# Three edits to a fused convolution and attention block on one core: the order of small steps at the front, the last eviction of a convolution by images, and tiles of their own for the input side during attention

## The chip, the core and the metric

The kernel runs on one core of one Trainium2 chip. The metric is the device time of one execution in microseconds; the time before is 2306.33 us, the median of three runs (2305.39 to 2307.38). All data are float32.

## The reference

The input x has 8 images of 512 channels and 32 x 32 points. A group normalisation (32 groups of 16 channels) comes first, then a block with N = 2 bottlenecks, and x is added to the result. C is 256, there are 4 heads of 64 channels, `cbs` is a convolution, a batch normalisation with given statistics and a silu.

```python
t = cbs(x, cv1_w, cv1_bn, 0)                      # 1x1, 512 -> 512
ys = [t[:, :C], t[:, C:]]
for i in range(N):
    yi = ys[-1]
    z = cbs(yi, m_cv1_w[i], m_cv1_bn[i], 1)       # 3x3, 256 -> 256
    z = bot_attention(z, m_qkv_w[i], m_rw[i], m_rh[i])
    z = silu(bn_eval(conv2d(z, m_cv2_w[i], 0), m_cv2_bn[i]))
    ys.append(yi + z)
return cbs(concatenate(ys, axis=1), cv2_w, cv2_bn, 0)
```

`bot_attention` projects z to q, k and v, adds a position term `rw + rh` to k, and takes a softmax over the 1024 points of an image for each head: `softmax(q (k + r) / 8) v`.

## The kernel before

Images are handled in four pairs (p = 0 to 3), image a and image b of a pair. For a pair and each of the two bottlenecks n, one 3x3 convolution covers both images; then the attention of image a runs, then that of image b. Behind the attention of one pair lie the group normalisation and the first convolution (cv1) of the next pair; the last convolution (cv2) closes a pair.

**Order of the instructions.** The program is written stage by stage, and a planner puts each engine's instructions in an order before the run: an instruction written earlier goes first where it is ready in the planner's own model of time. [...] `tc.issue_after(ins)` adds an edge: what is written under it comes after `ins` on the engine of `ins`. Tiles of one tag share a fixed number of places (`bufs`); a new tile waits until the readers of the tile whose place it takes are done, DMAs among them.

**Front** (lines 1507 to 1594). The statistics of the first image's channels come in two parts: `bn_stats` on VectorE (`gn_stats`, L653) for the first half, and ScalarE passes with an accumulator (`stats_by_act`, L686) for the second half and for the whole second image. The three small steps between those passes (L700, L702, L703: the mean, and both sums divided by 1024) run on VectorE. `group_norm_part` (L705) then averages over groups on TensorE (gm_ps, gv_ps), forms gr and shift on VectorE and GpSimd, and applies them on ScalarE (L724). Beside that, `make_u` (L381) turns the 3x3 filters into Winograd form: for each of three row stages i three tiles u_new, with two copies on ScalarE (L404, L405) and six or nine steps on VectorE (L388 to L411), then a store by GpSimd's queue (L415). Three of the eight filter blocks are made into tiles of the tag `pt` by `u_new_early` (L375); `pt` has six places. The batch-norm scales sh and bh are made on VectorE at L1553 to L1558 from rstd, a power on GpSimd (L1549), ahead of the second image's statistics.

**Input side of a convolution** (`tiles_in`, L490). It takes the padded image yp to Winograd form in three stages i. A stage has a row tile (w_ba or w_g, or two w_ec), w_rows with two fills of its borders by GpSimd (L520, L521), w_d, w_ab, and three results (v_in, or v_new which is then stored in DRAM). All its work is on VectorE, lines 511 to 558. w_ba, w_g, w_rows and w_d take the tag `acc`, which has two places and also holds the running sums of the softmax.

**Convolution** (`conv3x3`, L561). For each half oc of the output channels and each of three stages i, TensorE makes the products into two PSUM tiles (`ps_big` has three); ScalarE copies one part (m24, L607), and nine steps on VectorE (L612 to L644) give rows of z for both images at once. After the third stage a silu (L648) runs over z in four pieces, image by image. The projections (`project_strassen`, L840, or `project_direct`, L792, for p = 0) of image a start on oc = 0 and need oc = 1 of image a next.

**Attention** (`attention_fast`, L940). It has four groups (two channel halves by two halves of the points) of four pairs of steps each. For a pair: logits on TensorE (l_ps, L963), two exponentials on ScalarE (L967), two additions on VectorE (L981, L983), and, one pair later, the products with v (av_ps, L997). A group ends with s_ps (L1014), the eviction (L1004 on ScalarE, L1005 on VectorE) and a scaling (L1069). Other work is hung behind these steps by `behind`: the key (g, j) stands for pair j of group g, the key g for pair 0, and what hangs there is written after the additions of the following pair. `NORM_A` and `NORM_B` list the keys at which one step of the next normalisation runs (in this order: statistics of four channel blocks, the mean, gr and shift, then the applications). In the first bottleneck's attention of image b, `NORM_B` and one stage of `tiles_in` of image a hang there; another stage runs before it. With `at_once` the last group is scaled directly at the end (L1107 to L1115), and the product m_ps (L1195) waits for that.

## Time and profile before

| what | value |
|---|---|
| median of three runs | 2306.33 us |
| profiled execution | 2304.68 us |
| its span, first to last instruction | 2302.9 us |
| granted TensorE clock, mean | 0.993 |
| DMA, mean over the span | 122 GB/s |
| first row tile of the input side starts | 65.08 us |
| first product of the first convolution | 79.70 us |
| first product of the first attention | 152.30 us |

The profile is one execution. Its lines give for each engine when an instruction started, how long it took, and in brackets how long the engine had been idle just before it and which instruction released it. `x<-y` means that tile x was written from tile y, and L967 is line 967 of the kernel. The view of waits adds these idle times up by pair of waiting and releasing line: sum, number, longest. A table by stages gives the busy time of each engine in the order TensorE, weight loads, VectorE, ScalarE, GpSimd, then the granted TensorE clock, the DMA share and GB/s.

The slices of the span show where the engines are less than full: TensorE is at 6 and 7 tenths in the first two of forty slices (57.6 us each) and 7 in the last, and 9 or more elsewhere. VectorE is at 6, 9 and 8 in the first three.

### The profile page before, as it was taken

How to read it: one execution, taken by the hardware profiler on the slowest of the kernel's cores; microseconds unless marked ns; L12 is line 12 of the kernel's file. 1: busy time of each engine (PE TensorE's matmuls, PEld its weight loads, DVE VectorE, ACT ScalarE, POOL GpSimd, SP SyncE). 2: the span in 40 equal slices, each digit the busy share in tenths (PEclk: the TensorE clock that was granted, in tenths of full speed). 3: DMA queues.
4: the chain of work that ended last, by engine and by line, in shares of the span. 5: the costliest groups of instructions: out<-in, count | busy, mean ns of one | idle time of the engine just before them, and what ended most of it. 6: DMA issues, size and time to landing. Idle time of an engine off the chain costs nothing.

```text
span 2302.9 us, 40466 instructions
## 1 busy us (share of the span) xinstructions
PE 2216.4 (96%) x16338; PEld 1081.5 (47%) x16338; DVE 1750.1 (76%) x2640; ACT 1089.1 (47%) x1336; POOL 212.3 (9%) x417
## 2 busy tenths in 40 slices
PE   6799999999999999999999999999999999999997
PEld 3553437443465443734347443564345733473443
DVE  6987888778758689886857868986794868886742
ACT  7245462545225665365323665445622454335533
POOL 4113200000120000000021000000012000000002
PEclk9899999999999999999999999999999999999999
DMA  8634616321473232613158141442126611251114
GB/s 309 216 112 132 258 52 226 121 74 64 106 225 137 79 120 79 216 47 96 52 144 271 33 155 53 147 145 75 57 71 173 226 47 57 60 196 41 49 28 134
DMA packets 127892, 281.06 MB, mean 122 GB/s; under 512 B 34096, under 2 KB 55324, under 8 KB 126672
## 3 DMA queue, kind: packets, MB, share of 16 engines
q1 hardware_dynamic: 99712, 192.25, 25.6%
q0 software_dynamic: 27984, 86.13, 12.4%
q8 instruction: 131, 2.15, 0.4%
q14 instruction: 65, 0.53, 0.1%
HBM read 210.29 MB, written 68.03 MB: 121 GB/s over the span
## 4 chain that ended last, share of the span: by engine, by line
PE 78%; DVE 13%; ACT 4%; issue 2%; DMA 2%; POOL 1%; DVEq 0%; SPq 0%; ACTq 0%; POOLq 0%
PE av_ps L997 16%; PE l_ps L963 15%; PE c L1215 8%; PE c_ps L602 8%; PE c_new L1215 6%; PE p_ps L853 6%; PE ps L485 5%; PE m_ps L1195 4%; PE x_ps L1315 4%; PE pv_ps L859 2%; DVE acc L983 2%; ACT pt L967 1%; PE s_ps L1014 1%; PE p_ps L859 1%; DVE acc L981 1%
## 5 line engine op out<-in xcount | busy, mean ns | idle before, releaser
L967 ACT ACTIVATE pt<-l_ps 128x1024 f32<-128x1024 f32 x512 | 495.2, 1023 | 341.0 <-PE l_ps L963 303.6
L983 DVE TENSOR_TENSOR acc<-acc,pt 128x1024 f32<-128x1024 f32 x384 | 469.6, 1223 | 85.4 <-ACT pt L967 62.4
L963 PE MATMUL l_ps<-q,kr 64*64 64x512 f32 x4096 | 488.3, 591 | 10.1 <-ACT pt L967 7.7
L997 PE MATMUL av_ps<-pt,vT 64*64 64x512 f32 x4096 | 486.4, 592 | 7.5 <-DVE z L1005 5.0
L963 PEld LDWEIGHTS l_ps<-q,kr 64*64 64x64 f32 x4096 | 157.6, 133 | 280.7 <-issue 247.0
L997 PEld LDWEIGHTS av_ps<-pt,vT 64*64 64x64 f32 x4096 | 154.9, 133 | 281.8 <-issue 238.9
L602 PEld LDWEIGHTS c_ps<-v_in,u 128*64 128x64 f32 x4320 | 235.7, 137 | 5.3 <-issue 5.3
L602 PE MATMUL c_ps<-v_in,u 128*64 128x128 f32 x4320 | 237.5, 273 | 0.0
L1195 PE MATMUL m_ps<-z,m_sb 128*128 128x512 f32 x256 | 114.9, 600 | 6.2 <-DVE z L1069 6.2
L607 ACT COPY c_m<-c_ps 128x512 f32<-128x512 f32 x48 | 28.2, 587 | 185.3 <-PE c_ps L602 84.0
L853 PE MATMUL p_ps<-t_z,sq 128*128 128x512 f32 x224 | 107.0, 595 | 0.0
L981 DVE TENSOR_TENSOR acc<-pt 128x1024 f32<-128x1024 f32 x64 | 77.9, 1217 | 32.1 <-ACT pt L967 32.1
L853 PE MATMUL p_ps<-z,sq 128*128 128x512 f32 x168 | 80.4, 605 | 8.2 <-ACT z L458 8.2
L458 ACT ACTIVATE t<-m_ps,bh,sh 128x512 f32<-128x512 f32 x64 | 46.3, 774 | 82.7 <-PE m_ps L1195 82.7
L1195 PEld LDWEIGHTS m_ps<-z,m_sb 128*128 128x128 f32 x256 | 48.2, 191 | 66.7 <-issue 55.5
L1265 POOL DMA_DIRECT2D c_out<-in_x_dram x56 | 50.4, 974 | 312.4 <-ACT c_out L458 309.3
L520 POOL MEMSET w_rows<- 128x32 f32 x48 | 7.9, 165 | 635.0 <-PE s_ps L1014 376.9
L1005 DVE TENSOR_TENSOR z<-av_ps,z 128x512 f32<-128x512 f32 x64 | 44.0, 687 | 26.3 <-ACT z L1004 26.3
L458 ACT ACTIVATE c_out<-cz,bh,sh 128x512 f32<-128x512 f32 x14 | 16.7, 1296 | 90.7 <-DVE cz L1292 90.7
L1069 DVE TENSOR_TENSOR z<-z,rs 128x512 f32<-128x512 f32 x64 | 43.8, 684 | 20.1 <-DMA rs<-r_dram 19.7
L485 PE MATMUL ps<-x,w 128*128 128x512 f32 x128 | 56.1, 594 | 0.0
L1315 PE MATMUL x_ps<-t_x,sw 128*128 128x512 f32 x128 | 55.9, 592 | 0.0
(322 smaller groups left out, 3168.7 us busy)
## 6 DMA issues: line engine op xcount, KB each, us to landing
u<-u SPq DMA_DIRECT2D x135, 512.0 KB
sq<-sq SPq DMA_DIRECT2D x42, 384.0 KB
rs<-r_dram SPq DMA_DIRECT2D x118, 128.0 KB
x<-in_x_dram SPq DMA_DIRECT2D x28, 512.0 KB
r_in<-r SPq DMA_DIRECT2D x28, 512.0 KB
y_in<-y SPq DMA_DIRECT2D x28, 512.0 KB
c_out<-in_x_dram POOLq DMA_DIRECT2D x56, 256.0 KB, 5.2
out_dram<-c_out POOLq DMA_DIRECT2D x56, 256.0 KB, 3.8
```

What stands on the lines that cost most here:

```text
L485: last_product[0] = nc.tensor.matmul(ps[:, half, :], w_of(k), rhs_of(k, half), start=(k == begin), stop=(k == end))
L602: nc.tensor.matmul(to[o], us[cp][:, k, row, c, o], rhs, start=(k == 0), stop=(k == NM - 1),)
L853: nc.tensor.matmul(ps[:, o, :], w[:, o, :], rhs, start=not onto, stop=True, skip_group_check=onto)
L859: nc.tensor.matmul(v[:, ts(j, P)], rhs[:, ts(j, P)], w[:, 2, :], start=j == 0 and not onto, stop=True, skip_group_check=True,)
L963: nc.tensor.matmul(ps[kh * HD : (kh + 1) * HD, hd, :], kr[r, c, o : o + HD], q[r, c, ts(half, HALF)], start=True, stop=True,)
L967: last_exp[0] = exp = nc.scalar.activation(pt, ps, AF.Exp, scale=SCALE)
L981: return nc.vector.tensor_tensor(accs[g], pt[0], pt[1], ALU.add)
L983: ins = nc.vector.tensor_tensor(accs[g], accs[g], pt[i], ALU.add)
L997: nc.tensor.matmul(avs[g][hd * HD : (hd + 1) * HD, kh, :], vT[r, j, o : o + HD], pt[i][r, hd, :], start=(j == 0), stop=(j == NJ - 1),)
L1195: nc.tensor.matmul(pss[half][:, oc, :], m2_sb[:, n, k, ts(oc, P)], ao[:, k, ts(half, HALF)], start=(k == 0), stop=(k == NM - 1),)
L1215: nc.tensor.matmul(ps[:, o, :], w[:, k, ts(o, P)], rhs[part][:, c], start=(k == 0 and not onto), stop=(k == KB - 1), skip_group_check=onto,)
L1315: nc.tensor.matmul(ps[:, o, :], w[:, c, ts(o, P)], rhs[c], start=(c == 0 and not onto), stop=(c == 1), skip_group_check=onto,)
```

## The change

It has these parts.

- bnp moves from a tile of its own to one of two places of the tag `h`.
- `u_new_early` puts two filter tiles in one tile of the tag `pt`.
- In `stats_by_act` the three small steps run on ScalarE.
- In the front, the second image's statistics are written before the steps that make sh and bh; its applications from the second channel block on come after the latest filter copy (`behind_u`), and three further filter steps are written between them.
- In `conv3x3`, the eviction of the last stage of the last channel half is written per image, followed by that image's silu.
- In the first bottleneck's attention of image b, the input side's tiles take the tags `p3` and `p4` (one place each). Its last stage hangs at (2, 1) in place of 1; in the last pair its middle stage hangs at (1, 1) in place of before the attention.
- One key of `NORM_B`, (1, 3), becomes (1, 1), so that the mean and gr come one step earlier; for p = 0 the list `NORM_A` loses (1, 3) and gains (3, 1), so that what comes after the four statistics moves one step later.
- After that attention, the sums of the next cv1 except the first, and the input side's first stage, come after the last scaling.
- ScalarE's filter copies in the first attention of p = 0 come after the latest exponential, those of the block made during its projection after the last silu.

```diff
-    bnp = const.tile([P, NBN, 4], F32, name="bnp")
+    bnp = act.tile([P, NBN, 4], F32, tag="h", name="bnp", bufs=2)
...
     def u_new_early():
-        return act.tile([P, 2, 2, P], F32, tag="pt", name="u_new", bufs=6)
+        if not halves_of_u:
+            both = act.tile([P, 2, 2, 2, P], F32, tag="pt", name="u_new", bufs=6)
+            halves_of_u.extend((both[:, 1], both[:, 0]))
+        return halves_of_u.pop()
...
-            nc.scalar.copy(u5, c2)
+            copied_u[0] = nc.scalar.copy(u5, c2)
...
-                e = act.tile([P, 2 * NT * NM, F + 2], F32, tag="acc", name="w_rows", bufs=2)
+                e = room("w_rows", [P, 2 * NT * NM, F + 2])
...
-                d = act.tile([P, 4, 2 * NT * NM * NT], F32, tag="acc", name="w_d", bufs=2)
+                d = room("w_d", [P, 4, 2 * NT * NM * NT])
...
+                    final = i == NI - 1
+                    parts = groups if final and oc == NM - 1 else 1
+                    n_q = q // parts
...
+                    for part in range(parts):
+                        qs, tl, xs_ = ts(part, n_q), ts(part, n_q // NT), ts(part, 4 * n_q)
...
+                        tt(m[:, :, 0::2], slots(inner_ps, 0)[..., qs], m24[..., qs], ALU.add)
+                        tt(m[:, :, 1::2], slots(inner_ps, 0)[..., qs], m24[..., qs], ALU.subtract)
...
+                        if final:
+                            stt(dst[:, 0, tl], tiles(r0), -6.0, tiles(big_s[:, xs_]), ALU.mult, ALU.add)
+                            stt(dst[:, 3, tl], tiles(r1), -6.0, tiles(big_d[:, xs_]), ALU.mult, ALU.add)
+                            per = groups // parts
+                            for g in range(part * per, (part + 1) * per):
+                                for half in range(NH):
+                                    z_part = z[:, oc, g, ts(half, HALF)]
+                                    last_silu = silu(z_part, z_part, bn_m1[n] + oc)
...
-            nc.vector.tensor_scalar(mean, total, -1.0 / HW, None, ALU.mult)
+            nc.scalar.activation(mean, total, AF.Identity, scale=-1.0 / HW)
             each(AF.Square, square, bias=mean)
-            nc.vector.tensor_scalar(mv[:, :, 0], total, 1.0 / HW, None, ALU.mult)
-            nc.vector.tensor_scalar(mv[:, :, 1], square, 1.0 / HW, None, ALU.mult)
+            nc.scalar.activation(mv[:, :, 0], total, AF.Identity, scale=1.0 / HW)
+            nc.scalar.activation(mv[:, :, 1], square, AF.Identity, scale=1.0 / HW)
...
+                ahead = behind(c)
...
+                    with tc.issue_after(ahead.ins) if ahead else nullcontext():
+                        applied = nc.scalar.activation(
...
-            def sums():
+            def sums(after=None):
                 kept["t"] = t1, t2, t3, t4 = [t_tile() for _ in range(4)]
                 for c in range(2):
                     tt(t1[:, c], b12[c], b11[c], ALU.subtract)
-                for c in range(2):
+                with tc.issue_after(after.ins) if after else nullcontext():
+                    for c in range(2):
...
+    def behind_u(c):
+        if c == 2:
+            for _ in range(3):
+                next(chunk)
+        return copied_u[0] if c else None
...
+    with tc.issue_after(made.ins), tc.issue_after(applied.ins):
+        norm = s.group_norm_part(xs_second, by_act=True, behind=behind_u)
+        next(norm)
+        for made in chunk:
+            pass
     with tc.issue_after(made.ins):
         nc.vector.tensor_tensor(sh, bnp[:, :, 0], rstd, ALU.mult)
...
-    with tc.issue_after(last.ins), tc.issue_after(applied.ins):
-        norm = s.group_norm_part(xs_second, by_act=True)
-        next(norm)
-        for made in chunk:
-            pass
...
             def early():
-                for _ in make_u(1, 0, 0, first_taps, new=u_new_early):
-                    pass
+                with tc.issue_after(s.silued[0].ins):
+                    for _ in make_u(1, 0, 0, first_taps, new=u_new_early):
+                        pass
...
         def step_u():
-            return next(more_u, None)
+            with tc.issue_after(s.last_exp[0].ins):
+                return next(more_u, None)
...
-        NORM_B = ((0, 2), (0, 3), (1, 2), (1, 3), 2, (2, 1), (2, 2), (2, 3), 3, (3, 1), (3, 2), (3, 3))
+        NORM_B = ((0, 2), (0, 3), (1, 1), (1, 2), 2, (2, 1), (2, 2), (2, 3), 3, (3, 1), (3, 2), (3, 3))
...
+        if p == 0:
+            NORM_A = (*NORM_A[:4], 2, *NORM_A[6:], (3, 1))
...
+        def in_attention(name, shape):
+            return act.tile(shape, F32, tag="p4" if name == "w_rows" else "p3", name=name)
+
-        def tiles_later(i):
-            s.tiles_in(Y2[0], put_away, [i], ec)
+        def tiles_later(i, room=in_attention):
+            s.tiles_in(Y2[0], put_away, [i], ec, room)
             store(i)
...
-        with tc.issue_after(s.k_added[-2].ins) if direct else nullcontext():
-            tiles_later(1)
         if more:
+            with tc.issue_after(s.k_added[-2].ins) if direct else nullcontext():
+                tiles_later(1, None)
...
-        behind = hooks(NORM_B, (), {1: lambda: tiles_later(2)}) | {
+        behind = hooks(NORM_B, (), {}) | {
...
         if not more:
+            behind[1, 1] = lambda: tiles_later(1)
...
+        apply = behind[2, 1]
+        behind[2, 1] = lambda: (apply(), tiles_later(2))
         end = s.attention_fast(qkv, z[:, :, 1], at_of(ib, 0), behind, at_once=True)
         if more:
-            nxt.sums()
+            nxt.sums(end.scaled)
...
-        s.tiles_in(Y2[0], putter(vs, 0), [0])
+        with tc.issue_after(end.scaled.ins):
+            s.tiles_in(Y2[0], putter(vs, 0), [0])
```

## The prediction, made before the result was known

> **What bounds the kernel now.** I read the page first, then TensorE's waits, then the timelines around the longest of them.

> ```profile
> PE 2216.4 (96%) x16338; PEld 1081.5 (47%) x16338; DVE 1750.1 (76%) x2640; ACT 1089.1 (47%) x1336; POOL 212.3 (9%) x417
> ...
> PE 78%; DVE 13%; ACT 4%; issue 2%; DMA 2%; POOL 1%; DVEq 0%; SPq 0%; ACTq 0%; POOLq 0%
> ```

> TensorE is busy for 96% of the span, and the change removes no matmul. So only TensorE's idle time, 2302.9 − 2216.4 = 86.5 us, can be won, and some 15 us of it is the tail after the last large product (2288.0 to 2302.9). From the view of waits:

> ```profile
> PE p_ps L853 <- ACT z L458: 8.2, 7, 1.2
> ...
> PE c_ps L602 <- ACT c_m L607: 7.5, 1, 7.5
> PE m_ps L1195 <- DVE z L1069: 6.2, 3, 2.5
> PE c_ps L602 <- DVE v_in L557: 5.9, 1, 5.9
> ```

> Two long single waits, 7.5 and 5.9 us, belong to the first convolution; one of 1.2 us comes back in seven convolutions. The timelines of VectorE and TensorE in the front show what is behind the long ones:

> ```profile
> 37.82 0.28 PE L663 MATMUL gm_ps<-mv,gmat 64*64 64x4 f32 x4 [2.45 <-DVE mv L702]
> ...
> 42.31 0.17 DVE L703 TENSOR_SCALAR mv<-square 128x4 f32<-128x4 f32 x1 [3.12 <-ACT junk L697]
> ...
> 58.84 0.42 DVE L406 TENSOR_TENSOR u_new<-taps 128x256 f32<-128x256 f32 x1 [6.23 <-DMA u<-u_new]
> ...
> 71.78 1.21 DVE L511 SCALAR_TENSOR_TENSOR w_ba<-ypad 128x1024 f32<-128x1024 f32 x1
> ...
> 103.35 0.68 DVE L613 TENSOR_TENSOR c_t<-c_ps,c_m 128x512 f32<-128x512 f32 x1
> ...
> 104.18 9.38 PE L602 MATMUL c_ps<-v_in,u_new 128*64 128x128 f32 x128 [7.48 <-ACT c_m L607]
> ```

> The times are starts, the bracket is the idle time before. VectorE stands still for 6.23 us because all six filter tiles wait to be stored; from 58.84 on it has no gap worth naming, and TensorE's third group starts right after its eviction at 103.35. The table by stages confirms it:

> ```profile
> 59.00:79.70 20.70, 20.63 (x49) 8.83 (x48) 20.42 (x43) 7.62 (x11) 6.45 (x16) 1.00 0.71 245
> 79.70:104.20 24.50, 11.11 (x162) 10.68 (x162) 24.19 (x50) 3.50 (x4) 1.74 (x8) 0.81 0.60 207
> ```

> VectorE (third figure) is full in both; TensorE (first) is at 11.11 of 24.50 in the second. This stage is VectorE's.

> **Part 1, the front.** Two filters in one tile double the places for new filters from 6 to 12: the 6.23 us go. The means and scalings on ScalarE take L700, L702, L703 from VectorE's queue: the 3.12 us go, and TensorE's 2.45. The batch-norm steps L1553 to L1558 move behind the second image's filters; VectorE waited 1.79 us for GpSimd's power (L1549) before them. Together VectorE could be 6.23 + 3.12 + 1.79 = 11.1 us earlier. What is late next: the second image's input side, L511 at 71.78, needs Y1[1], which ScalarE finishes at 65.94 + 2.29 = 68.23. That chain gains less. ScalarE's squares start when the mean is there (37.64 before; 35.2 + 0.2 after), so the evictions that free the fourth product's PSUM come about 2.4 us earlier, 65.8 for Y1[1]. So the gain is 71.78 − 65.8 = 6.0 us if VectorE idles there, and up to 10 if the planner puts the next stage of the first image ahead. I take 7.5: in the trace only two small steps (L515) are put ahead. TensorE's own start at 79.7 moves to 77.3, so it isn't the bound.

> [...] In the trace a small step is 0.16 to 0.17 us on VectorE (L700 to L703), the nearest ScalarE row is 0.20 (L472, 128x1). [...]

> The filter copies placed between the second image's applications (two per filter stage, 0.3 us each) make its later channels up to 1.4 us later; TensorE needs 1.7 us per channel and ScalarE gives one in 1.5, so this is covered. The stores that these steps issue (0.54 us each on GpSimd) come behind gr and shift; only places for filters wait for them, and of those there are 12. bnp in a work buffer costs nothing: its last reader ends at 31.3, the first other user of that tag (L554) starts at 69.83. Without that cover it would be one wait of under 1 us.

> **Part 2, last eviction by images,** in eight convolutions:

> ```profile
> 964.69 0.68 DVE L644 SCALAR_TENSOR_TENSOR z<-c_r,c_k 128x512 f32<-128x512 f32 x1
> ...
> 966.27 3.70 PE L853 MATMUL p_ps<-z,sq 128*128 128x512 f32 x8 [1.17 <-ACT z L458]
> ```

> The nine steps from 960.83 to 965.37 take 4.54 us. Queued steps start 0.60 us apart at 512 elements and 0.34 at 256, so 128 should take about 0.2: three at 0.34, four at 0.2, two at 0.34, and 0.1 for the dependences, 2.6 us. Image 0 is ready 1.9 us earlier, more than the wait of 1.17 (1.63 in the first convolution). If the planner slips steps of image 1 into the gaps, as it does with L981 between L555 and L557, each costs 0.34. Bounds per convolution: 0.3 and 1.17; I take 1.0 of 1.17 and 1.4 of 1.63: 7 × 1.0 + 1.4 = 8.4 us. [...]

> **Part 3, sums and tiles behind the last scaling** (p = 1 and 2; in p = 0 and 3 no wait stands there):

> ```profile
> 901.56 0.62 DVE L548 TENSOR_TENSOR w_d<-w_rows 128x512 f32<-128x512 f32 x1
> 902.10 0.67 DVE L1069 TENSOR_TENSOR z<-z,rs 128x512 f32<-128x512 f32 x1
> ...
> 902.83 4.38 PE L1195 MATMUL m_ps<-z,m_sb 128*128 128x512 f32 x6 [2.51 <-DVE z L1069]
> ```

> Ahead of this scaling stand six steps L1349 to L1351 and four of the input side, 10 × 0.6 = 6.0 us. Without them the row of sums (ScalarE, ready at 893.0), its addition (0.6) and the reciprocal (3.3) set its start, about 897.2; TensorE would be ready at 900.3. So 2.51 us go, twice: 5.0. The moved steps are needed from 914 on.

> **Part 4, first attention of p = 0.** It waits 1.08 us (l_ps at 177.51, an exponential behind filter copies L404, L405), 1.81 (gm_ps at 185.56), 1.26 and 1.19. Copies behind the last exponential and the mean one step later remove the first two, 2.9; I take 2.5, as the applications move by one step too. The first filter's four copies behind the last silu (0.3 us each) cost nothing: ScalarE idles 2.01 us ahead of L827 at 142.09.

> **Part 5, attention of the second image, n = 0.**

> ```profile
> 312.56 1.09 PE L963 MATMUL l_ps<-q,kr 64*64 64x512 f32 x8 [0.47 <-DVE gr L682]
> ...
> 318.17 1.09 PE L963 MATMUL l_ps<-q,kr 64*64 64x512 f32 x8 [1.94 <-ACT pt L967]
> ...
> 1926.19 1.09 PE L997 MATMUL av_ps<-pt,vT 64*64 64x512 f32 x8 [1.52 <-ACT pt L967]
> ...
> 1964.57 0.64 PE L1014 MATMUL s_ps<-acc,ones 128*32 128x256 f32 x8 [0.95 <-DVE acc L983]
> ```

> In p = 0, 1, 2 each 0.28 + 0.47 + 1.94 + 0.25 = 2.94 us: gr stands behind the input side's steps, so two applications run back to back ahead of an exponential. In p = 3 1.52 + 0.67 + 1.30 + 0.95 + 1.01 = 5.45. The change reads gr one step earlier and gives the input side own tiles, at step (2, 1), in p = 3 also (1, 1). But its steps (1.13 + 1.2 + 1.2 + 0.67 + 0.6 + 3 × 0.67 with L551/L552 and L557/L558, about 6.2 us) now follow the additions of pair (2, 2) and stand ahead of those of (2, 3); s_ps and L1005 of the next group wait for those. Laid on p = 3's rows: the exponentials of (2, 2) end at 1954.5, their additions at 1955.7, the burst at 1961.9, the additions of (2, 3) at 1964.2; s_ps was due at 1963.6, and L981 and L1005 still follow: 1 to 2 us late. The nearest row is p = 3 itself, where a like burst one step earlier gave 0.95 + 1.01 = 1.96. Bounds for a burst: 0 and 4. I take 1.9: gain 3 × 1.0 and 5.45 − 2 × 1.8 = 1.9, together 4.9. On GpSimd's queue the burst's two fills (0.16 us each) and three stores (0.54) go behind gr and shift, ahead of which they stood (store at 312.73, gr at 313.28).

> **Sum.** 7.5 + 8.4 + 5.0 + 2.5 + 4.9 = 28.3 us. The profiled execution took 2304.7 (span 2302.9 and 1.8 around it), so 2276.4; the median of the runs lies 1.6 above it: 2278.0.

> **The rivals.**
> - *All waits go.* The planner fills VectorE's gap (front 10) and bursts slip between additions (part 5 gives 14.3 − 3): 10 + 9.8 + 5.0 + 2.9 + 11.3 = 39: 2267. For it: VectorE has 5 us to spare in a group of 14.5. Against: priority follows the program.
> - *Bursts replace the waits.* Parts 4 and 5 give nothing and the interleaving halves part 2: 7.5 + 4.9 + 5.0 = 17.4: 2289.
> - *The change doesn't do what it says:* the planner's order undoes the front and the split alike; only some waits go: 2304.
> - *Slower.* Each of the five bursts hits in full: 6.2 us, then L981 1.13 and L1005 0.6 behind it, 7.9 × 5 = 39.5 on top of the old waits, against 7.5 + 8.4 + 5.0 + 2.5 = 23.4: 2322. It decides from 23.4 / 5 = 4.7 us per burst; against it, p = 3 shows 2.

> **How the numbers follow.** Forecast 0.58, all waits 0.17, bursts replace 0.19, undone 0.03, slower 0.03. Measurement can tell about 0.2% (4.6 us) from no change: faster 0.94, same 0.03, slower 0.03. Range 2266 to 2292: both neighbours with their bounds; left out are the last two and the edges, under 0.2.

> **What would show it.** Right: no DMA wait before L406 in the front, third group near 96.7; the wait of p_ps for z under 0.2; m_ps without 2.51. New waits of s_ps and av_ps one pair after step (2, 1) of about 1 us each. Wrong: VectorE still full of one-image steps when z is due, or a filter wait that merely moved to the inputs' tiles, or attention waits above 4 us per burst.

## The result, and the profile after

The changed kernel takes 2297.99 us in the median of 11 runs (2295.83 to 2301.12), the kernel before in the same series 2305.69 (2303.85 to 2308.10). The ratio is 0.9968, with a 95% interval of 0.9959 to 0.9977: faster by 7.7 us, where 28.3 were forecast. The profiled execution took 2295.83, the fastest of the eleven, with a span of 2294.2 against 2302.9.

The first line of the page gives each engine's busy time:

```profile
PE 2217.6 (97%) x16338; PEld 1083.3 (47%) x16338; DVE 1755.7 (77%) x2706; ACT 1090.1 (48%) x1342; POOL 208.6 (9%) x417
```

TensorE has the same 16338 matmuls and the same busy time within 1.2 us, so the whole gain is in idle time. The view of TensorE's waits in the changed kernel (us in total, times, longest) says which idle time went and which came:

```profile
PE av_ps L1016 <- DVE z L1024: 10.7, 10, 2.4
...
PE s_ps L1033 <- DVE acc L1002: 7.2, 6, 1.5
PE ps L490 <- ACT ypad L463: 7.0, 2, 5.2
PE pv_ps L878 <- ACT u_zv L907: 4.8, 7, 0.7
PE p_ps L872 <- DVE c_t L633: 3.1, 7, 1.1
```

The rows aimed at are gone or small: p_ps for z (8.2), m_ps for z (6.2), l_ps for gr (0.2 of 1.4) and most of l_ps for pt. But other rows are new or have grown. Evictions in the front cost 7.0 instead of 0.7; the seven projections now wait for u_zv and for a PSUM tile (4.8 + 3.1); s_ps waits for acc 7.2 instead of 1.0, and av_ps for z 10.7 instead of 5.0.

The front before, ScalarE and TensorE:

```profile
42.78 4.23 ACT L458 ACTIVATE ypad<-ps,bh,sh 128x512 f32<-128x512 f32 x4
46.79 5.72 ACT L724 ACTIVATE x_second<-x_second,shift,gr 128x512 f32<-128x512 f32 x8
...
52.00 27.63 PE L485 MATMUL ps<-x_second,w_first 128*128 128x512 f32 x64
```

The same place, from the timelines of ScalarE, TensorE and VectorE in the changed kernel:

```profile
38.93 2.21 ACT L463 ACTIVATE ypad<-ps,bh,sh 128x512 f32<-128x512 f32 x2
...
43.79 2.93 ACT L743 ACTIVATE x_second<-x_second,shift,gr 128x512 f32<-128x512 f32 x4 [2.65 <-POOL shift L737]
...
51.27 2.20 ACT L463 ACTIVATE ypad<-ps,bh,sh 128x512 f32<-128x512 f32 x2
...
53.52 29.12 PE L490 MATMUL ps<-x_second,w_first 128*128 128x512 f32 x64 [5.19 <-ACT ypad L463]
...
71.18 1.23 DVE L520 SCALAR_TENSOR_TENSOR w_ba<-ypad 128x1024 f32<-128x1024 f32 x1 [8.42 <-ACT ypad L463]
...
103.11 9.36 PE L611 MATMUL c_ps<-v_in,u_new 128*64 128x128 f32 x128 [7.71 <-ACT c_m L616]
```

VectorE was relieved as forecast: it stands idle for 8.42 us. What it waits for is late. ScalarE does two evictions, stands still 2.65 us for the shift, does all the applications, and only then, at 51.27, the two evictions that free TensorE's next PSUM tile. Those two could have run in the 2.65 us, as their products ended at 39.18; ScalarE ran them in the place that its list gives them, behind the applications. TensorE therefore pauses 5.19 us ahead of x_second. The third group starts at 103.11 instead of 104.18.

A projection behind a convolution (p = 1, n = 1), where the wait for z of 1.17 us was:

```profile
956.13 0.94 PE L878 MATMUL pv_ps<-sq,t_z 128*128 128x128 f32 x6 [0.68 <-ACT u_zv L907]
...
957.26 0.41 DVE L660 SCALAR_TENSOR_TENSOR z<-c_r,c_k 128x256 f32<-128x256 f32 x1
...
958.16 1.95 PE L872 MATMUL p_ps<-t_z,sq 128*128 128x512 f32 x4 [1.10 <-DVE c_t L633]
```

Image 0's z is written at 957.67, and nobody waits for it any more. TensorE waits for the PSUM tile instead, which image 1's L633 has yet to read.

In the second image's attention (p = 0) the burst's price shows at the two places that were worked out, with 1.5 and 1.0 us where about 1 us each was forecast:

```profile
319.72 0.64 PE L1033 MATMUL s_ps<-acc,ones 128*32 128x256 f32 x8 [1.48 <-DVE acc L1002]
321.37 1.95 PE L1016 MATMUL av_ps<-pt,vT 64*64 64x512 f32 x16 [1.01 <-DVE z L1024]
```

Setting TensorE's start of each stage against before gives the account by place: front and first split -1.06; first attention of p = 0 as a whole 0; second image's attentions -0.92, -0.98, +0.58, -1.12; m_ps of p = 1 and 2 with the products just behind -4.47 (-4.27 at the end of the block) and -2.78; the projections of n = 1 in p = 1 and 2 +1.16 each, the other projections 0. In p = 0 the first image's attention of n = 1 loses 0.71 (s_ps waits 0.72 for acc at 465.96); the forecast has no term for it, and its cause stays open.

### The profile page after: what moved, and what is told of

Its sections match the earlier page's. It is cut to its first block, busy times and chain, and to the rows that moved or that the text cites. A ratio compares the mean times of both kernels' runs of the same rounds, so it can differ in the third digit from the quotient of the medians.

```text
span 2294.2 us, 40531 instructions
## 1 busy us (share of the span) xinstructions
PE 2217.6 (97%) x16338; PEld 1083.3 (47%) x16338; DVE 1755.7 (77%) x2706; ACT 1090.1 (48%) x1342; POOL 208.6 (9%) x417
## 3 DMA queue, kind: packets, MB, share of 16 engines
q8 instruction: 131, 2.15, 0.4%
## 4 chain that ended last, share of the span: by engine, by line
## 5 line engine op out<-in xcount | busy, mean ns | idle before, releaser
L1016 PE MATMUL av_ps<-pt,vT 64*64 64x512 f32 x4096 | 489.2, 595 | 11.0 <-DVE z L1024 10.7
L1024 DVE TENSOR_TENSOR z<-av_ps,z 128x512 f32<-128x512 f32 x64 | 44.0, 688 | 19.7 <-ACT z L1023 19.7
L463 ACT ACTIVATE z<-z,bh,sh 128x512 f32<-128x512 f32 x64 | 47.8, 805 | 21.4 <-DVE z L660 21.4
```

The costliest lines, as they stand in the source:

```text
L463: silued[0] = nc.scalar.activation(dst, src, AF.Silu, scale=sh[:, k : k + 1], bias=bh[:, k : k + 1])
L1016: nc.tensor.matmul(avs[g][hd * HD : (hd + 1) * HD, kh, :], vT[r, j, o : o + HD], pt[i][r, hd, :], start=(j == 0), stop=(j == NJ - 1),)
```

## The experiments

Theory: two parts moved a wait, because what TensorE needs next comes from a list or a place that the change also touched, ScalarE's order in the front and PSUM tiles behind the convolutions. The rivals are those of the forecast: bursts on VectorE eat the gain, or the parts never did what they say. First each part was put alone on the kernel before, then causes were taken away one by one. Lines in rows are those of each variant's own file. All ratios are to the kernel before.

**split_only.** The kernel before with Part 2's loop over images alone.

> The kernel before with Part 2 alone (last eviction of a convolution by images). The forecast gave it 8.4 us: 2297.3. My theory now: image 0's z comes 1.9 us earlier, but the two PSUM tiles of the last group are freed only by image 1's steps at L633 and L635, about 4.5 us after the matmuls instead of 2.6, and the second product of the projection needs one of them. The wait for z (1.17) becomes a wait for a PSUM tile of about the same length, so the time stays within 1.5 us of before (2304 to 2307). If the loss came from another part of the change instead, this kernel is near 2297.

Measured 2305.97 against 2305.31, ratio 1.0004 (0.9996 to 1.0012). Part 2 alone shows no gain. Its waits are 7 x 0.68 for u_zv and 7 x 0.2 for c_t (the PSUM tile), in place of 7 x 1.17 for z, and in the first convolution 2.05 for c_t in place of 1.63 for z.

**front_only.** The kernel before with Part 1 alone.

> The kernel before with Part 1 alone (twelve places for new filters, small steps on ScalarE, batch-norm steps behind the second image's filters). The forecast gave it 7.5 us: 2298.2. My theory now: VectorE comes about 10 us earlier to the second image's input side and then stands about 8 us for Y1[1], because ScalarE's list now has the applications of the second image (L743) ahead of two evictions of the first image that were ready; TensorE's x_second products then wait about 5 us for a PSUM tile. Expected -1 us, 2304 to 2305.5, with a start of the first convolution 2.5 to 3 us later than before and its third group 1 us earlier.

Measured 2304.92 against 2305.31, ratio 0.9999 (0.9992 to 1.0007). ScalarE's list is that of the changed kernel (evictions at 39.78 and 51.32, applications from 43.84), VectorE stands 7.03 us for Y1[1]. The first convolution starts 1.54 us later than before (2.5 to 3 were expected) and its third group 2.4 us earlier (1 was expected). So the front shows no gain by itself, without the other parts.

**sums_behind_scaling.** The kernel before with Part 3 alone:

```diff
-            nxt.sums()
+            nxt.sums(end.scaled)
...
-        s.tiles_in(Y2[0], putter(vs, 0), [0])
+        with tc.issue_after(end.scaled.ins):
+            s.tiles_in(Y2[0], putter(vs, 0), [0])
```

> The kernel before with Part 3 alone (sums of the next cv1 and the first input tiles behind the last scaling). The forecast gave it 5.0 us: 2300.7. In the changed kernel m_ps came 4.27 and 2.78 us earlier in p = 1 and 2, and 1.16 and 1.15 were lost at the projection behind the next convolution, where VectorE begins the last eviction 0.9 us later after the end of the matmuls. If that loss belongs to this part, the sum is -7.05 + 1.9 to 2.3 = about -5 us (2300.7), with a longer wait for z in those two convolutions. If it belongs to the split, the sum is -7 us (2298.7) and the wait for z stays at 1.17.

Measured 2301.48, ratio 0.9985 (0.9978 to 0.9991). In its trace the m_ps blocks end 4.27 and 2.78 us earlier, and the projections of n = 1 behind them lose 0.87 and 0.90: VectorE, with the moved steps still to do, starts the last eviction 2.15 us after the end of the matmuls instead of 1.27 (p = 1). So most of the loss of 1.16 in the changed kernel is Part 3's own; in split_only the same place loses 0.28.

**own_tiles_only.** The kernel before with Part 5 alone, and bnp in a work buffer to make room.

> The kernel before with Part 5 alone (own tiles for the input side, its place in the second image's attention, the mean one step earlier), and the batch-norm's input in a work buffer, without which the tiles don't fit. The forecast gave it 4.9 us: 2300.4. From the changed kernel's TensorE: -0.92, -0.98, +0.58 and -1.12 in p = 0 to 3, so -2.4: 2302.9. If the burst were harmless and the loss of p = 2 came from elsewhere: -4: 2301.3.

Measured 2303.54 against 2306.06, ratio 0.9987 (0.9980 to 0.9994): 2.5 us. In p = 2 its attention gains 0.98, with the same waits of 1.41 and 1.01 in it. The loss there in the changed kernel's trace thus doesn't come from the burst's waits alone (see the last section).

**copies_behind_exp.** The kernel before with Part 4 alone:

```diff
-                for _ in make_u(1, 0, 0, first_taps, new=u_new_early):
-                    pass
+                with tc.issue_after(s.silued[0].ins):
+                    for _ in make_u(1, 0, 0, first_taps, new=u_new_early):
+                        pass
...
-            return next(more_u, None)
+            with tc.issue_after(s.last_exp[0].ins):
+                return next(more_u, None)
...
+        if p == 0:
+            NORM_A = (*NORM_A[:4], 2, *NORM_A[6:], (3, 1))
```

> The kernel before with Part 4 alone (filter copies behind the last exponential, other steps of the mean in the first attention of p = 0). The forecast gave it 2.5 us: 2302.8. From the changed kernel: waits of 0.63, 1.16 and 2.37 in the place of the old ones, so 0 at the end of this attention: 2305.3.

Measured 2306.00 against 2306.06, ratio 0.9998 (0.9991 to 1.0004). The waits of 1.08, 1.81 and 1.26 (4.15 together) are replaced by 0.65, 1.16 and 2.37 (4.18).

**split_reads_whole.** The kernel before with another split: the steps that read PSUM stay whole, only the steps in SBUF go by images. Set against the split of the change:

```diff
+                    tt(m[:, :, 0::2], slots(inner_ps, 0), m24, ALU.add)
+                    tt(m[:, :, 1::2], slots(inner_ps, 0), m24, ALU.subtract)
...
+                    whole_m, whole_e = m, e
                     for part in range(parts):
-                        tt(m[:, :, 0::2], slots(inner_ps, 0)[..., qs], m24[..., qs], ALU.add)
...
```

> The kernel before with another split: the three steps that read PSUM (L612, L613, L614) stay whole for both images, only the six SBUF steps and the silu behind them go image by image. z of image 0 comes at 3 x 0.60 + 4 x 0.20 + 2 x 0.34 = 3.3 us after the copy instead of 4.5, PSUM is freed as before. If the PSUM tiles decide, the wait of 1.17 goes in seven convolutions and 1.2 of 1.63 in the first: about -8 us, 2297 to 2299. If the planner's order or VectorE's load decides instead, it gains as little as the split of the change, under 2 us.

Measured 2305.01, ratio 0.9996 (0.9988 to 1.0004). My theory of the PSUM tile as the one cause fell: the tile is free in time, the wait for z is 0.18, and still no gain shows. The timelines show the next in line (p = 1, n = 1; ScalarE before, then TensorE and ScalarE of this run):

```profile
964.25 1.01 ACT L890 COPY m_z<-p_ps 128x1024 f32<-128x1024 f32 x1 [0.34 <-PE p_ps L853]
...
967.07 1.98 PE L863 MATMUL p_ps<-z,sq 128*128 128x512 f32 x4 [0.18 <-ACT z L458]
...
969.13 1.28 ACT L472 ACT_TABLE_LOAD   x1
...
970.54 0.99 ACT L900 COPY m_z<-p_ps 128x1024 f32<-128x1024 f32 x1
...
971.58 1.13 PE L863 MATMUL p_ps<-z,sq 128*128 128x512 f32 x2 [0.82 <-ACT m_z L900]
```

Since the silus can start earlier, the planner puts all four, and the load of the exponential's table (1.28 us), ahead of the copy of m_z. In the kernel before this copy stood ahead of the silus, at 964.25. TensorE's next product goes into the tile that this copy reads.

**split_whole_table_later.** The same, with the table load behind the copy of q in seven projections:

```diff
-            with tc.issue_after(last_silu.ins):
-                table_of(AF.Exp)
+            if table:
+                with tc.issue_after(last_silu.ins):
+                    table_of(AF.Exp)
...
-            nc.scalar.copy(q0, ps_a[:, 0])
+            q0_copied = nc.scalar.copy(q0, ps_a[:, 0])
+            if table:
+                with tc.issue_after(q0_copied.ins):
+                    table_of(AF.Exp)
```

> As the split with whole PSUM reads, and one more edit: in the seven convolutions followed by a projection in seven products, the load of the exponential's table (1.28 + 0.20 us on ScalarE) is moved from behind the last silu to behind the copy of q (L907). In the run without this edit the wait for z fell from 8.2 to 1.3 us, but TensorE then waited 7 times 0.82 us for the copy of m_z, which stood on ScalarE behind four silus and that table load; the sum came out at 0. If a chain of covered waits decides (z, then a PSUM tile, then ScalarE), taking the table load out of ScalarE's list frees m_z 1.5 us earlier, the 0.82 go, and the gain is that of Part 2 in the forecast: 7 x 1.0 to 1.17 and about 1 in the first convolution, 2297 to 2299. If ScalarE's four silus alone hold it up, or yet another wait comes up behind, less than 3 us.

Measured 2298.37 against 2306.06, ratio 0.9963 (0.9950 to 0.9977): 7.7 us. In its trace every one of the seven projections is 0.96 to 1.00 us shorter than before:

```profile
963.76 0.99 ACT L901 COPY m_z<-p_ps 128x1024 f32<-128x1024 f32 x1
...
966.28 1.88 PE L864 MATMUL p_ps<-z,sq 128*128 128x512 f32 x4
```

The copy of m_z follows the silus at once, and the product behind it has no bracket. Three waits lay on top of one another; the gain comes when the last is gone.

**table_later_only.** The control: the table load moved, the eviction whole.

> The kernel before, its last eviction whole, with the table load alone moved behind the copy of q in seven convolutions. A control: in the kernel before the copy of m_z stands ahead of the silus, so nothing waits for the table load, and the wait for z (1.17) stays. Expected 0, 2305 to 2307. If the table load was the whole of it and the split gives nothing, -7.

Measured 2305.12 against 2306.25, ratio 0.9997 (0.9988 to 1.0005). Neither moving the table load without the split nor this split without it shows a gain.

**after_evict_first.** The changed kernel, with two evictions of the first image ahead of the second image's applications:

```diff
-        return copied_u[0] if c else None
+        return copied_u[0] if c else evicted_1
...
+    y0s = new_y0()
+    with tc.issue_after(squared[0].ins):
+        s.cv1(w1_of, xs, y0s, Y1[0], Y_ORDER[:2], begun)
+    evicted_1 = s.silued[0]
...
-    s.cv1(w1_of, xs, y0s, Y1[0], Y_ORDER, begun)
+    s.cv1(w1_of, xs, y0s, Y1[0], Y_ORDER[2:], begun)
```

> The changed kernel with one edit in the front: the two evictions of the first image's second output block are written ahead of the second image's applications, and these are issued behind them. My theory: ScalarE uses the 2.65 us in which it waits for the shift, the PSUM tile is free at 43.3, TensorE's wait of 5.19 goes, x_second starts at about 48.5 instead of 53.5 and Y1[1] is ready at about 66 instead of 71.2. VectorE's idle time of 8.42 shrinks by as much, and the third group comes 5 us earlier: 2293 (2291.5 to 2294.5). Rival: VectorE's or POOL's list, or the filters' stores, hold the input side as late as before, and the time stays at 2298.

Measured 2291.65 against 2306.06, ratio 0.9935 (0.9922 to 0.9949): 14.4 us, where the changed kernel has 7.7. Its rows of ScalarE, TensorE and VectorE:

```profile
38.41 4.16 ACT L463 ACTIVATE ypad<-ps,bh,sh 128x512 f32<-128x512 f32 x4
42.65 2.96 ACT L743 ACTIVATE x_second<-x_second,shift,gr 128x512 f32<-128x512 f32 x4
...
47.64 27.63 PE L490 MATMUL ps<-x_second,w_first 128*128 128x512 f32 x64
...
63.83 1.23 DVE L520 SCALAR_TENSOR_TENSOR w_ba<-ypad 128x1024 f32<-128x1024 f32 x1 [1.13 <-ACT ypad L463]
...
95.76 9.62 PE L611 MATMUL c_ps<-v_in,u_new 128*64 128x128 f32 x128 [7.72 <-ACT c_m L616]
```

The hole of 2.65 us is filled, x_second starts 5.88 us earlier than in the changed kernel and without a pause, Y1[1] is ready at 63.8, the third group starts at 95.76. The forecast said 65.8 and 96.7. What had held the gain back was the list that the planner made.

**evict_first_vector_steps.** The kernel of after_evict_first with the statistics' small steps (mean, two scalings) back on VectorE. The wait in question is the 3.12 us of VectorE ahead of L703 and the 2.45 of TensorE in the rows of before; the steps' own time is 0.16 to 0.17 us there, and 0.19 on ScalarE in the changed kernel (L717, L719, L720).

> The changed kernel with the repaired list in the front, and the statistics' small steps (mean, two scalings, for both halves of the first image's and the second image's channels) back on VectorE. [...] If the wait counts, the squares start about 2.5 us later, x_second and the third group too: 2293.5 to 2294.5. If only their own time counts, 2291.5.

Measured 2293.00, ratio 0.9950 (0.9936 to 0.9963). This interval overlaps that of the run before; the traces differ by 2.17 us at the first attention (146.34 against 144.17), with VectorE's part of the chain late again (gv_ps waits 1.13 for dev). The squares start at 35.89 instead of 33.47, so in these traces the wait counts and not the steps' own time. The size is not shown: the medians don't tell the two kernels apart, and in evict_first_table_later and best_three_parts below, which have the same edits in the front, x_second starts at 50.22 and 49.33, behind sixteen matmuls that took 8.83 and 8.72 us (7.13 in the kernel before and in the changed kernel), where it is 47.64 in after_evict_first and 49.65 here.

**after_two_halves.** The changed kernel, with the input side's steps in the second image's attention cut in two, at (2, 1) and (2, 2).

> The changed kernel with the input side's steps in the second image's attention cut in two: differences and rows at step (2, 1), the rest at (2, 2). In the changed kernel the whole burst stands ahead of the additions of pair (2, 3), and s_ps then waits 1.48 us and av_ps 1.0, some 2.5 us in each of four attentions. If the burst's length ahead of those additions decides, the wait for acc (4 x 1.4) goes and part of the one for z: -5 to -9 us, 2289 to 2293. If VectorE's total work in this group decides, the second half only moves the delay to the eviction of z (L1024), and the gain is under 2.5 us.

Measured 2300.03 against 2306.25, ratio 0.9974 (0.9965 to 0.9984): no gain over the changed kernel. The wait of s_ps is gone; the one of av_ps has taken it over (TensorE, then VectorE):

```profile
320.92 1.95 PE L1022 MATMUL av_ps<-pt,vT 64*64 64x512 f32 x16 [2.68 <-DVE z L1030]
...
320.18 0.68 DVE L1030 TENSOR_TENSOR z<-av_ps,z 128x512 f32<-128x512 f32 x1
```

2.68 is about the sum of the 1.48 and 1.01 of the changed kernel: the second half stands ahead of the eviction of z.

**after_three_parts.** In three parts, none ahead of both the additions before s_ps and that eviction:

```diff
+                    with tc.issue_after(s.z_done[0].ins):
+                        next(steps)
...
-        apply = behind[2, 1]
-        behind[2, 1] = lambda: (apply(), tiles_later(2))
+        spread_tiles(2, ((2, 1), (2, 3), (3, 1)))
```

> The changed kernel with the input side's steps in the second image's attention cut in three: rows (3.0 us) at step (2, 1), differences and the first product's tiles (1.9 us) behind the eviction of z of group 2, the rest (2.0 us) at (3, 1); in p = 3 also the earlier burst, at (1, 1), (1, 3) and 2. If the place decides, the waits of s_ps (1.4) and av_ps (1.0) go in five groups, some 2.4 us each, and the last s_ps waits up to 0.8 us longer: -8 to -12 us, 2286 to 2290. If VectorE's total work decides, it only moves again and the time stays within 3 us of 2298.

Measured 2290.60 against 2306.37, ratio 0.9930 (0.9916 to 0.9943): 15.8 us against 7.7, so 8.1 better than the changed kernel, at the lower end of what the place should give. The last s_ps pays 0.91 to 1.92 us, most of it new and more than the 0.8 I allowed, and in p = 3 one wait for z of 1.01 is left. So it is the place, with some rest of VectorE's work.

**evict_first_table_later** joins the front's repaired list and the split of split_whole_table_later, in the changed kernel.

> The changed kernel with the repaired list in the front (evictions ahead of the applications) and, in place of its split, the split with whole PSUM reads and the table load behind the copy of q. The front alone came to 2291.7. My theory adds the parts: in the changed kernel the split gained 0 in five convolutions, lost 1.16 in two and gained 0 in the first; the other split gained 1.0 in seven and 1.2 in the first on the kernel before. In the two convolutions where Part 3 delays the eviction by 0.9 us it should cover about the same 1.0 to 1.26. So 7 x 1.0 + 1.2 + 2 x 0.3 = 8.8 us off 2291.7: 2283 (2281 to 2285). If the parts don't add because VectorE is late in the changed kernel, 2287 or more.

Measured 2283.02 against 2306.25, ratio 0.9898 (0.9883 to 0.9914). That is what the sum of the two causes gives (2283).

**best_three_parts** adds the three parts.

> The changed kernel with all three repairs: evictions ahead of the applications in the front, the split with whole PSUM reads and the table load behind the copy of q, the input side in three parts. The first two came to 2283.0. If the three parts gain what they gain alone and the causes are independent, 2271 to 2275; if VectorE's work decides, 2281 to 2284.

Measured 2275.09 against 2306.37, ratio 0.9865 (0.9850 to 0.9880): 31.3 us, near the 28.3 forecast for the change, though it took three repairs that the change doesn't have. TensorE's idle time over 0.2 us a piece is 44.4 us, against 60.9 in the changed kernel and 71.2 before.

## Why the prediction was wrong, step by step

| part | forecast | alone on the kernel before | with its obstacle removed |
|---|---|---|---|
| 1 front | 7.5 | 0.4 | 6.7 more than the changed kernel |
| 2 last eviction by images | 8.4 | -0.7 | 7.7 (other split, table later) |
| 3 sums and tiles | 5.0 | 3.8 | |
| 4 first attention, p = 0 | 2.5 | 0.1 | not tried |
| 5 second image's attention | 4.9 | 2.5 | 8.1 more than the changed kernel |

Differences of medians, in us, each to the kernel before of its own series; the last column sets 14.4 and 15.8 against 7.7. Of the parts alone, those of 1, 2 and 4 are not told from zero; 3 and 5 have intervals of 2.1 to 5.1 and 1.4 to 4.6. The five parts alone sum to 6.1; the change has 7.7.

- **Part 1** failed at "so the evictions that free the fourth product's PSUM come about 2.4 us earlier, 65.8 for Y1[1]". That VectorE is freed, that Y1[1] is next and that 6 us or more are in reach, all held (6.7 came with the repaired list). But I moved the evictions along with the squares as if ScalarE's list stayed as it was. The first two came 3.85 us earlier (42.78 to 38.93); the next two went behind eight applications and ended at 53.5 instead of 47.0. Y1[1] was ready at 71.15, later than the 68.23 of before. TensorE's start, called "77.3, so it isn't the bound", was 82.57, behind a pause in the products that feed Y1[1].
- **Part 2** failed at "Image 0 is ready 1.9 us earlier, more than the wait of 1.17". I asked what frees z, not what else TensorE's next products need. The split that makes z early makes the PSUM tile late (L633 ends 5.4 us after the matmuls, against 2.6 for L613); and when that is mended, ScalarE's copy of m_z is late. The slip of an image 1 step into the gaps, which I did foresee, cost 0.33 us (L632 at 956.60), and nobody waited for it. The sum of 8.4 takes nothing off for VectorE's added work. The spacing of the steps in the trace gives 2 × 2.6 − 4.54 = 0.7 us per convolution as an estimate; in split_only 72 more steps cost 4.6 us of busy time, 0.6 per convolution, and in p = 1 and 2 some of it shows in the time, 0.28 us each.
- **Part 3** was right in mechanism: m_ps lost its wait of 2.51 in both places. Its size was 4.27 in p = 1, because in the kernel before the six products behind the pause also took 4.38 us instead of 2.84 (below). "The moved steps are needed from 914 on" missed that they delay the next eviction on VectorE: 0.87 and 0.90 given back. Without the slowdown the terms are 2 x 2.78 - 1.77 = 3.8, which is the measured difference of medians.
- **Part 4** failed at "remove the first two, 2.9; I take 2.5". They went; the exponential at 198.12 now stands behind an application and two filter copies, and the eviction of z at 202.47 behind filter steps (1.16 and 2.37). The sum stayed and the place changed. The forecast had taken off only 0.4 us for what the moved steps would stand ahead of.
- **Part 5** was right in its mechanism and too large in its sum. A burst cost 2.4 to 2.5 us in p = 0 to 2 where 1.9 was taken, and the attentions gained 0.9 to 1.1, except in p = 2 of the changed kernel, where the clock fell (0.53 from 1428.70 to 1432.10), and in p = 3 of own_tiles_only. The term of p = 3 was 1.9, and it brought 1.1; with the 1.9 per burst that the text takes it would have been 1.65, as the sum uses 1.8 there. The burst's listed steps add up to 6.8 and not to 6.2; in the changed kernel's p = 0 it took 6.4.

Of the rivals, *the change doesn't do what it says* had the nearest time (2304), and for the front and the split its mechanism: they were undone, the front by the planner's order, the split by PSUM and then by that order. *Bursts replace the waits* (2289) put the price in the wrong place, as the bursts cost little more than forecast. I gave the former 0.03 because I took the order of the kernel before for granted, although the lists are planned anew from written order and readiness. The move of the small steps to ScalarE was right as far as two traces show: the steps took 0.19 us there against 0.16 to 0.17 on VectorE, and the wait counted.

## What to carry to other kernels

When a planner orders the lists, a step that becomes ready earlier can overtake a step that TensorE needs more: work out the new list of each engine that the change touches, not just the new time of the step. Before crediting a removed wait, write down everything the waiting engine needs for its next three instructions (operand, PSUM tile, the copy that frees it) and when each is there; the gain reaches only to the second latest of them. If a part shows 0 alone, look for the wait that took its place: here three of them were one or two edits away, and together these edits were worth 31.3 - 7.7 = 23.6 us.

## What the runs showed of the hardware

- Behind some pauses TensorE ran at half its clock for 3.41 us (0.50 from 903.99 to 907.40 in the kernel before, and from 52.94 to 56.35 in the changed kernel). Around the 5.19 us ahead of 53.52 the clock fell: it was 0.59 in the next 3.5 us, and the 64 matmuls took 29.12 us instead of 27.63, so the pause cost 1.5 us more than its length. In the kernel before, the six matmuls behind the pause of 2.51 at 902.83 took 4.38 us, and 2.84 behind an equal pause at 1458.06, where the clock did not fall (1.00). In the changed kernel it fell at the two pauses in p = 2's attention (0.53 from 1428.70 to 1432.10; sixteen matmuls 3.51 us instead of 1.95), which makes the +0.58 of that place, and at this one (0.50 from 203.13 to 206.54):

```profile
203.21 3.58 PE L1016 MATMUL av_ps<-pt,vT 64*64 64x512 f32 x16 [2.37 <-DVE z L1024]
```

```profile
900.58:903.99 3.41, 1.16 (x3) 1.00 0.02 5
903.99:907.40 3.41, 3.41 (x5) 0.50 0.00 0
...
1453.54:1456.95 3.41, 2.01 (x5) 1.00 0.01 1
1456.95:1460.36 3.41, 2.30 (x6) 1.00 0.00 0
1460.36:1463.78 3.42, 3.42 (x10) 1.00 0.00 0
```

The first pause lies almost whole in one stretch and leaves 1.16 us of work in it; the second is divided between two stretches, with 2.01 and 2.30 us of work. From 25 us on, in the two traces together, half the clock followed on all 10 full-clock stretches with TensorE busy for 0 to 1.43 us (up to 42%), on none of the 4 with 1.49 to 1.67 us (44 to 49%), and on none of the 1301 above half. In these traces a removed pause was thus worth its length or some 1.5 us more (29.12 − 27.63 = 1.49, 4.38 − 2.84 = 1.54, 3.51 − 1.95 = 1.56), and its place on the grid went with which.
- A fall of the clock moved a whole front. In copies_behind_exp, whose front is unedited and has the same lists up to the first convolution, twelve matmuls behind a pause of 2.46 us took 8.44 us at a granted clock of 0.50 and 0.61 (5.42 at 1.00 in the kernel before, behind 2.45), and the first convolution started 2.2 us later, at 81.90. A difference of 2 us in a front needs timed runs, not one trace.
- In the changed kernel's evictions (p = 1, n = 1, 954.79 to 959.52), VectorE's steps of 128 elements start 0.20 us apart (estimated at 0.2), those of 256 elements 0.33 to 0.34.
